# Two cross-attention layers on one core: key weights loaded in two parts, projections dealt out anew, and the layer-1-only units and the end in another order

## The chip, the cores and the metric

The kernel runs on one core of a Trainium2 chip. The metric is the device time of one execution in microseconds. Five engines work beside each other, each through its own instructions in order: TensorE (PE in the profile, with PEld for its weight loads), VectorE (DVE), ScalarE (ACT), GpSimd (POOL) and SyncE (SP), which here only issues DMAs. DMAs run in queues of the engines that issue them.

## The reference

Two attention layers follow each other, each with 20 heads of 16 channels, on x of shape 8 x 256 x 320 with a context of shape 8 x 256 x 512. A context of 256 rows has text rows and a few image rows (179 image rows in the first layer, 4 in the second), with projections of their own.

```python
# layer 0: text is enc[:, :77], ip is enc[:, 77:]
q = split(x @ Wq.T)
k, v = split(text @ Wk.T), split(text @ Wv.T)
k_ip, v_ip = split(ip @ Wk_ip.T), split(ip @ Wv_ip.T)
out = merge(attend(q, k, v)) + merge(attend(q, k_ip, v_ip))
x = out @ Wo.T + bo + x
# layer 1: text is enc[:, :252], ip is enc[:, 252:]
q = heads(x @ W_q)
probs_t = softmax(q @ k_t.T * scale)
text_out = probs_t @ v_t
qsem = l2norm(probs_t @ text)
fused = q @ k_ip.T * scale + 0.5 * (qsem @ l2norm(ip).T)
ip_out = (softmax(fused) * mask) @ v_ip
out = (text_out + ip_out) @ W_out + b_out + x
```

Layer 1 takes layer 0's result. All is float32.

## The kernel before, in words

**Tiling.** The 20 heads are taken as five quads of four heads (QUADS), for each of the eight batches. A unit of work n is one quad: n = 5 b + s for quad s of batch b in layer 0. Layer 1 follows six units behind (SHIFT), so for n from 6 to 39 a unit holds a quad of layer 0 and a quad of layer 1 (both_layers, L1078); units 40 to 45 hold layer 1 alone (layer_1, L1123); then l1_end (L863) finishes the last batch. Below, (b1, g4) is the unit with quad 4 of batch 1 in layer 0.

**Inside a unit.** Scores of four heads are 16 passes of TensorE (L342) into four PSUM tiles; the masked q that they take is made on GpSimd (qz, L332). VectorE takes the maxima (L483 for layer 0, L696 for layer 1), ScalarE the exps (L495, L711), TensorE transposes the probabilities (L380) back into the same PSUM tiles, and VectorE or ScalarE copies them out (et, L387). Layer 0 then multiplies with v (L513). Layer 1 multiplies, one unit later, with a Gram matrix of the context beside v (l1_values, L722, matmuls L735 and L738), in two PSUM tiles in turn; a product on VectorE (L742) gives the norm that l2norm needs, and a small copy (L746, "num") takes the values out. Only when both are done may the PSUM tile be written again. The scores on the four image rows are copied from the score tiles before the transposes overwrite them (aip, L691).

**Norms and the fused softmax.** Once a batch, l1_norm (L766) takes a square root on ScalarE (L773) and then calls a dummy Exp (L776), each of which brings a load of an activation table; l1_fused, l1_fused_exp (L794), l1_probs and l1_probs_T (L828, L835) follow.

**What sets the order.** PE, DVE, ACT and POOL are under a manual schedule: each engine executes in the order in which the program calls. The projections are dealt into the units by fillers(n, place) (L976): a table maps a pair (s, place) to a list of calls. In both_layers place 0 lies behind the exps of heads 0 and 1 of layer 0 and ahead of those of heads 2 and 3 (behind both where the flag late is set), place 1 behind the first two transposes, places 2 and 3 around the values of layer 1, place 4 between the exps of the two pairs of layer 1, place 5 and 6 among its transposes. In layer_1 places 2 and 3 follow the two halves of the first loop, place 4 the image scores, 5 and 6 the transposes. The projections are project_q (L275, with an ACT copy L282), project_k (L293; for the third column chunk ACT makes eight copies, L451 to L457), project_rows for v (L305), l1_gram (L604), l1_k (two ACT copies, L575 and L576) and the out-projections (L318).

**Loads.** At the start ACT's queue loads wq, wk, wkip, their last 64 columns again (load_tail), wv and wvip, in this order; SP's queue loads x and the context; the later weights come through POOL's queue (load_late).

**The end.** l1_end multiplies the last quad's values and finishes the last batch; its image softmax is taken in two parts, heads 0 to 15 (first) and 16 to 19 (last), then the sums of the heads are transposed (text), the image part is added (image), and the out-projection follows (project, L905).

## Time and profile before

| what | us |
|---|---|
| median of the runs before (3 runs: 904.05 to 906.41) | 904.2 |
| the profiled execution | 902.27 |
| its span, first to last instruction | 900.6 |
| PE busy | 867.4 |
| first scores of the first unit start | 14.89 |
| last unit with its end (866.89 to 900.60) | 33.71, PE busy 25.31 |
| a layer-1-only unit (832.02 to 842.41) | 10.39, PE busy 9.43 |

The mean granted clock of TensorE was 0.997. A line of the timeline gives the start, the duration, the engine, the line, the operation, the tiles written and read with their shapes, the count, and in brackets how long the engine was idle before it and what ended that. A line of the windows gives a stretch, its length, the busy time of PE, PEld, DVE, ACT and POOL with their counts, PE's granted clock, the busy share of the DMA engines and GB/s.

### The profile page before, as it was taken

The page shows a single profiled execution, that of the slowest core. Times are in us where ns is not written, and L with a number is a line of the kernel's source. Part 1 is how long each engine was busy: PE and PEld are TensorE (multiplying, and loading weights), DVE is VectorE, ACT ScalarE, POOL GpSimd, SP SyncE. Part 2 cuts the span into 40 slices and gives each one's busy share as a digit, 9 for nine tenths or more (in the row PEclk, how much of TensorE's full clock was granted, in tenths as well). Part 3 has the DMA queues.
Part 4 walks back from the last instruction along what each step waited for, and adds up shares of the span by engine and source line. Part 5 has one row for each costly group of instructions (what it writes and reads, how often), then busy time and mean ns, then how long its engine had stood idle before and what let it go on. Part 6 is the DMA issues. An engine that isn't in the chain of part 4 may idle for free.

```text
span 900.6 us, 18697 instructions
## 1 busy us (share of the span) xinstructions
PE 867.4 (96%) x6170; PEld 696.6 (77%) x6170; DVE 606.3 (67%) x2043; ACT 550.1 (61%) x2406; POOL 221.8 (25%) x397
## 2 busy tenths in 40 slices
PE   6999899999999999999999999999999999899996
PEld 4767678788777888788887788878877887678774
DVE  1454477767776777776777677776687767874664
ACT  3775666646654686556766468555775557745663
POOL 5522311213211232132221223212221223212201
PEclk9999999999999999999999999999999999999998
DMA  9500100001000100001001010001000100000000
GB/s 298 143 6 1 56 2 1 1 16 42 15 2 21 33 24 2 20 17 42 15 1 21 16 43 1 1 20 34 24 1 11 25 1 2 1 20 1 1 20 16
DMA packets 21072, 22.96 MB, mean 25 GB/s; under 512 B 5856, under 2 KB 20128, under 8 KB 20976
## 3 DMA queue, kind: packets, MB, share of 16 engines
q1 hardware_dynamic: 15072, 13.27, 5.8%
q10 hardware_dynamic: 4608, 4.38, 1.6%
q0 software_dynamic: 1296, 4.12, 1.5%
q8 instruction: 50, 0.82, 0.4%
q14 instruction: 46, 0.38, 0.1%
HBM read 18.31 MB, written 2.62 MB: 23 GB/s over the span
## 4 chain that ended last, share of the span: by engine, by line
PE 80%; ACT 6%; DVE 2%; issue 1%; POOL 0%; ACTq 0%; DVEq 0%
PE y L735 15%; PE sc L380 15%; PE sc L342 8%; PE v L305 8%; PE y L738 8%; PE k L293 6%; PE q L275 6%; PE p_o L318 5%; PE oT L513 4%; ACT e L495 2%; ACT e L711 2%; PE g L604 2%; PE p_aT_ps L311 1%; PE ipo L842 1%; PE o L533 1%
## 5 line engine op out<-in xcount | busy, mean ns | idle before, releaser
L495 ACT ACTIVATE e<-sc,nmx 128x77 f32<-128x77 f32 (+1 forms) x640 | 227.1, 411 | 57.5 <-DVE nmx L483 57.5
L711 ACT ACTIVATE e<-sc,nmx 128x252 f32<-128x252 f32 x320 | 147.0, 484 | 103.4 <-DVE aip L691 103.4
L735 PE MATMUL y<-gv,et 126*128 126x272 f32 x640 | 202.9, 398 | 5.0 <-ACT num L746 4.4
L742 DVE CUSTOM_DVE_ANT_0 e<-y,e 128x252 f32<-128x252 f32 x320 | 133.4, 418 | 108.2 <-PE y L738 96.4
L380 PE MATMUL sc<-ident,e 128*126 128x128 f32 (+1 forms) x1280 | 182.8, 275 | 11.8 <-ACT e L495 6.5
L483 DVE TENSOR_REDUCE nmx<-sc 128x2 f32<-128x154 f32 x320 | 109.6, 414 | 91.5 <-PE sc L342 91.5
L380 PEld LDWEIGHTS sc<-ident,e 128*126 128x126 f32 (+1 forms) x1280 | 148.1, 140 | 25.1 <-ACT e L495 12.5
L387 DVE COPY et<-sc 128x512 f32<-128x512 f32 (+1 forms) x222 | 149.9, 688 | 26.0 <-PE sc L380 16.8
L495 ACT ACTIVATION_READ_ACCUMULATOR e<-sc,nmx 128x1 f32 x640 | 159.7, 250 | 0.0
L738 PEld LDWEIGHTS y<-gv,et 126*128 126x128 f32 x640 | 121.1, 189 | 26.0
L738 PE MATMUL y<-gv,et 126*128 126x146 f32 x640 | 131.9, 288 | 0.0
L735 PEld LDWEIGHTS y<-gv,et 126*128 126x128 f32 x640 | 105.3, 191 | 22.7 <-ACT num L746 6.8
L548 POOL TENSOR_TENSOR attn<-o_sb 128x64 f32<-128x64 f32 x80 | 24.5, 327 | 396.9 <-DVE o_sb L538 357.0
L696 DVE TENSOR_REDUCE nmx<-sc 128x2 f32<-128x504 f32 x160 | 105.6, 673 | 24.2 <-PE sc L342 24.2
L387 ACT COPY et<-sc 128x512 f32<-128x512 f32 (+1 forms) x98 | 55.9, 587 | 75.4 <-PE sc L380 75.4
L342 PE MATMUL sc<-k,sc_qz 32*128 32x256 f32 x1152 | 83.4, 400 | 1.3 <-POOL sc_qz L332 0.8
L332 POOL TENSOR_SCALAR sc_qz<-q,quad_m 128x256 f32<-128x256 f32 x80 | 73.2, 926 | 10.2 <-ACT q L282 9.9
L342 PEld LDWEIGHTS sc<-k,sc_qz 32*128 32x128 f32 x1152 | 52.9, 184 | 24.7 <-issue 14.4
L711 ACT ACTIVATION_READ_ACCUMULATOR e<-sc,nmx 128x1 f32 x320 | 70.0, 219 | 0.0
L305 PE MATMUL v<-wv,encT 128*126 128x324 f32 (+1 forms) x192 | 58.1, 446 | 0.3 <-DMA wv<-in_WvT_dram 0.3
L318 PE MATMUL p_o<-wo,p_aT 128*128 128x320 f32 x180 | 52.8, 437 | 0.3 <-DVE p_aT L312 0.3
L746 DVE COPY num<-y 128x20 f32<-128x20 f32 x300 | 52.2, 174 | 0.0
(159 smaller groups left out, 1053.8 us busy)
## 6 DMA issues: line engine op xcount, KB each, us to landing
encT<-in_encT_dram SPq DMA_DIRECT2D x7, 512.0 KB
x<-in_x_dram SPq DMA_DIRECT2D x8, 320.0 KB
out_dram<-osb SPq DMA_DIRECT2D x15, 160.0 KB
xT<-in_xT_dram SPq DMA_DIRECT2D x7, 256.0 KB
texts<-in_encT_dram SPq DMA_DIRECT2D x6, 154.0 KB
xT<-in_xT_dram SPq DMA_DIRECT2D x7, 128.0 KB
vip_rows<-vipA SPq DMA_DIRECT2D x32, 25.0 KB
wk<-in_WkT_dram ACTq DMA_DIRECT2D x1, 640.0 KB
```

Source lines behind the costliest of these rows:

```text
L305: nc.tensor.matmul(ps, lhsT(k), w[:, k, :], start=(k == 0), stop=(k == NE - 1))
L318: nc.tensor.matmul(ps[:, :C], aT[:, m, :], w[:, m, :], start=(m == 0), stop=(m == NC - 1))
L342: nc.tensor.matmul(sc[j][:, half, :], qz[rows, half * P : (half + 1) * P], kT(j)[rows, :], start=True, stop=True,)
L380: nc.tensor.transpose(v[:, c, half, :], u["e"][x][:, i, half, t0 + c * tn : t0 + (c + 1) * tn], ident,)
L387: copy(u["et"][x][:tn, i].rearrange("p c n s -> p (c n s)"), ps)
L483: nc.vector.tensor_reduce(u["nmx"][x][:, j, :, a], u["sc"][2 * x + j][:, :, t0:t1], AX.X, ALU.max, negate=True,)
L495: nc.scalar.activation(u["e"][x][:, j, half, t0:t1], u["sc"][2 * x + j][:, half, t0:t1], AF.Exp, bias=u["nmx"][x][:, j, half, a : a + 1], ...
L696: nc.vector.tensor_reduce(u["nmx"][x][:, j, :], u["sc"][2 * x + j][:, :, t0 : t0 + TXT1], AX.X, ALU.max, negate=True,)
L711: nc.scalar.activation(u["e"][x][:, j, half, t0 : t0 + TXT1], u["sc"][2 * x + j][:, half, t0 : t0 + TXT1], AF.Exp, bias=u["nmx"][x][:, j, ...
L735: nc.tensor.matmul(y, et[:, 1 - odd, half, :], gv[0][:, g, full], start=True, stop=False)
L738: nc.tensor.matmul(y[:, into], et[:, odd, half, :], gv[1][:, g, part], start=False, stop=True)
L742: nc.vector.tensor_tensor_reduce(e, y[:, g0 : g0 + TXT1], e, op0=ALU.mult, op1=ALU.add, scale=1.0, scalar=0.0, accum_out=r["n2"][:, half, ...
```

## The change

Six things change.

1. wk and wkip become two tiles each: columns 0 to 127, and the rest with the 64 columns that are loaded again. The first parts (256 KB each) come on ACT's queue right after wq; wv, wvip and the rest of wk and wkip are issued on SP's queue. Four matmuls on zeros (8 passes) and a dummy Exp are put at the start.
2. (b1, g4) takes the last v projection of batch 2 at place 4; in (b2, g0) the third part of q moves from place 1 to place 0 in its stead.
3. In batches 2, 4 and 6 the second half of the next batch's l0_q moves from (3, 4) to (4, 0).
4. In the last batch (b = 7) the second Gram matrix moves from (2, 1) to (2, 4), the third part of l0_k from (2, 2) to (3, 0), the second l1_v from (3, 0) to (4, 0), the first l1_k from (40, 4) to (3, 4) and the second from unit 41 to unit 40. The flag late holds there for s = 4 and no longer for s = 3.
5. In layer_1 the first loop goes head by head: maximum, exp, product, with the copies shared differently. The transposes of heads 0 and 1 come ahead of the values of head 2. In the last unit l1_den is called ahead of the values of head 3.
6. In l1_end the copies of the first two heads' values go to VectorE, a dummy Sqrt is called ahead of the last two heads' values, the text matmuls come later, and the last transposed probabilities are copied by two engines.

```diff
@@ -117,10 +117,10 @@
         n = min(C, t.shape[2])
         eng.dma_start(out=t[:, :, 0:n], in_=w[:, 0:n].rearrange("(k p) c -> p k c", p=P))
 
-    def load_tail(t, w, eng):
+    def load_part(t, at, w, c0, c1, eng):
 
         eng.dma_start(
-            out=t[:, :, C:], in_=w[:, C - HP :].rearrange("(k p) c -> p k c", p=P)
+            out=t[:, :, at : at + c1 - c0], in_=w[:, c0:c1].rearrange("(k p) c -> p k c", p=P)
         )
 
     def load_xT(b, eng):
@@ -149,7 +149,11 @@
     wo, wo1 = new_c("wo"), new_c("wo1")
 
 
-    wk, wkip = new_e("wk", again=HP), new_e("wkip", again=HP)
+
+    wk, wkip = [
+        [const.tile([P, NE, n], F32, tag=f"{name}{n}", name=f"{name}{n}") for n in (P, C + HP - P)]
+        for name in ("wk", "wkip")
+    ]
     wk1 = const.tile([P, NE, C - HP], F32, tag="wk1", name="wk1")
 
     wv, wvip, wv1 = new_e("wv"), new_e("wvip"), new_e("wv1", again=NIP)
@@ -158,12 +162,23 @@
     bo_b = const.tile([P, C], F32, tag="bo_b", name="bo_b")
     bo1_b = const.tile([P, C], F32, tag="bo1_b", name="bo1_b")
     load_c(wq, WqT, nc.scalar)
-    load_e(wk, WkT, nc.scalar)
-    load_e(wkip, WkipT, nc.scalar)
-    load_tail(wk, Wk1, nc.scalar)
-    load_tail(wkip, Wk1, nc.scalar)
-    load_e(wv, WvT, nc.scalar)
-    load_e(wvip, WvipT, nc.scalar)
+    load_part(wk[0], 0, WkT, 0, P, nc.scalar)
+    load_part(wkip[0], 0, WkipT, 0, P, nc.scalar)
+    load_e(wv, WvT, nc.sync)
+    load_e(wvip, WvipT, nc.sync)
+    for w, given in ((wk, WkT), (wkip, WkipT)):
+        load_part(w[1], 0, given, P, C, nc.sync)
+        load_part(w[1], C - P, Wk1, C - HP, C, nc.sync)
+
+    zeros = work.tile([P, S], F32, tag="qz", name="zeros", bufs=2)
+    nc.vector.memset(zeros, 0.0)
+    ps = mm_tile("zeros")
+    for i in range(4):
+        nc.tensor.matmul(ps[:, :S], zeros[:, :P], zeros, start=True, stop=True)
+
+    one = small.tile([P, 1], F32, tag="one", name="one", bufs=1)
+    nc.vector.memset(one, 0.0)
+    nc.scalar.activation(one, one, AF.Exp)
 
     ident = const.tile([P, P], F32, tag="ident", name="ident")
     make_identity(nc, ident)
@@ -208,6 +223,8 @@
 
     def columns(w, k, m):
 
+        if isinstance(w, list):
+            w, m = (w[0], 0) if m == 0 else (w[1], m - 1)
         return w[:, k, m * P : (m + 1) * P]
 
     twice(wq)
@@ -690,9 +707,9 @@
         ip = 0 if u["t0"][x] else TXT1
         copy(bat[u["b"]]["aip"][:, :, h, :], sc[:, :, ip : ip + NIP])
 
-    def l1_max(u, x, image=True):
+    def l1_max(u, x, image=True, heads=range(2)):
         t0 = u["t0"][x]
-        for j in range(2):
+        for j in heads:
             nc.vector.tensor_reduce(
                 u["nmx"][x][:, j, :],
                 u["sc"][2 * x + j][:, :, t0 : t0 + TXT1],
@@ -703,9 +720,9 @@
             if image:
                 l1_image_scores(u, x, j, nc.vector.tensor_copy)
 
-    def l1_exp(u, x):
+    def l1_exp(u, x, heads=range(2)):
         t0 = u["t0"][x]
-        for j in range(2):
+        for j in heads:
             h = QUADS[u["g"]][1][2 * x + j]
             for half in range(NH):
                 nc.scalar.activation(
@@ -763,6 +780,11 @@
         nc.vector.reciprocal(by_head(r, "rden1", b)[:, :, hs], den)
         nc.vector.tensor_tensor(by_head(r, "nrm", b)[:, :, hs], den, den, ALU.mult)
 
+    def table(func):
+
+        one = small.tile([P, 1], F32, tag="one", name="one", bufs=1)
+        nc.scalar.activation(one, msk[:, 0:1], func)
+
     def l1_norm(b, hs=ALL):
         r = bat[b]
         n2 = r["n2"][:, :, hs]
@@ -771,9 +793,7 @@
         nc.vector.scalar_tensor_tensor(nrm, nrm, EPS2, n2, ALU.mult, ALU.max)
 
         nc.scalar.activation(nrm, nrm, AF.Sqrt, scale=1.0 / SEM_SCALE**2)
-
-        one = small.tile([P, 1], F32, tag="one", name=f"one_{b}", bufs=1)
-        nc.scalar.activation(one, msk[:, 0:1], AF.Exp)
+        table(AF.Exp)
 
     def l1_fused(b, hs=ALL, eng=nc.gpsimd):
         r = bat[b]
@@ -818,7 +838,7 @@
                 ALU.mult,
             )
 
-    def l1_probs_T(b, hs=ALL, ps=None):
+    def l1_probs_T(b, hs=ALL, ps=None, shared=False):
         r = bat[b]
 
         rows = hs.stop * NIP
@@ -832,7 +852,11 @@
             )
         if "pT" not in r:
             r["pT"] = small.tile([H * NIP, NH * P], F32, tag="pT", name=f"pT_sb_{b}", bufs=1)
-        nc.vector.tensor_copy(r["pT"][:rows], ps[:rows, : NH * P])
+        if shared:
+            for copy, cols in ((nc.vector.tensor_copy, slice(0, P)), (nc.scalar.copy, slice(P, 2 * P))):
+                copy(r["pT"][:rows, cols], ps[:rows, cols])
+        else:
+            nc.vector.tensor_copy(r["pT"][:rows], ps[:rows, : NH * P])
 
     def l1_attn(b):
         r = bat[b]
@@ -871,8 +895,9 @@
         def tile(j, name):
             return ps_sc.tile([P, NH * S], F32, tag=f"sc{j}", name=f"end_{name}")
 
-        def values(j, half):
-            l1_values(u, j, (half,), nc.scalar.copy)
+        def values(j, copy):
+            for half in range(NH):
+                l1_values(u, j, (half,), copy)
 
         def chunk(t, m):
             return t[:, CH[m] : CH[m] + P]
@@ -911,27 +936,23 @@
             for half in range(NH)
         ]
         o = [tile(2 + half, f"o_{half}") for half in range(NH)]
-        l1_den(b)
         l1_norm(b, first)
-        values(0, 0)
         l1_text(b, first)
-        values(0, 1)
+        values(0, nc.vector.tensor_copy)
         l1_fused(b, first)
-        values(1, 0)
-        values(1, 1)
+        values(1, nc.vector.tensor_copy)
         l1_fused_exp(b, first)
-        sums = tile(0, "aT")
-        text(sums, (0, 1))
-        values(2, 0)
-        values(2, 1)
+        table(AF.Sqrt)
+        values(2, nc.scalar.copy)
         l1_probs(b, first)
-        values(3, 0)
-        values(3, 1)
+        values(3, nc.scalar.copy)
         l1_norm(b, last)
         l1_text(b, last)
         l1_probs_T(b, first, tile(1, "pT"))
         l1_fused(b, last, nc.vector)
         l1_fused_exp(b, last, nc.vector)
+        sums = tile(0, "aT")
+        text(sums, (0, 1))
         image(sums, (0, 1), first)
         keep(sums, (0, 1))
         sums = mm_tile("end_aT2")
@@ -940,7 +961,7 @@
         project(0, 0)
         project(0, 1)
         project(1, 0)
-        l1_probs_T(b, last, tile(1, "pT2"))
+        l1_probs_T(b, last, tile(1, "pT2"), True)
         project(1, 1)
         image(sums, (2,), last)
         keep(sums, (2,))
@@ -1050,6 +1071,25 @@
                 },
             )[n]
             plan = {(s, at): f for at, f in plan.items()}
+        if b % 2 == 0 and b >= 2 and ahead < B:
+
+            plan[3, 4] = [(l0_q, ahead, (0,))]
+            plan[4, 0] = [(l0_q, ahead, (1,)), (l0_k, ahead, 0)]
+        if (b, s) == (1, 4):
+            plan[4, 4] = [(l0_v, ahead, 2)]
+        if (b, s) == (2, 0):
+            plan[0, 0], plan[0, 1] = plan[0, 1], []
+        if b == B - 1:
+
+            plan[2, 1] = [(l1_den, old), (l1_norm, old)]
+            plan[2, 2] = []
+            plan[2, 4] = [(l1_gram, now, 1), (l1_fused, old)]
+            plan[3, 0] = [(l0_k, now, 2)]
+            plan[3, 4] = [(l1_k, now, 0)]
+            plan[4, 0] = [(l1_v, now, 1)]
+        if b == B:
+            plan[0, 4] = [(l1_k, last, 1)]
+            plan[1, 4] = []
         for f, at, *args in plan.get((s, place), ()):
             if 0 <= at < B:
                 f(at, *args)
@@ -1082,7 +1122,7 @@
             l0_max(u0, pair)
         l0_exp(u0, 0)
 
-        late = n > NQ and n % NQ == 3
+        late = n > NQ and n % NQ == (3 if n < N0 - NQ else 4)
         if late:
             l0_exp(u0, 1)
         fillers(n, 0)
@@ -1131,21 +1171,21 @@
         if (n + 1 - SHIFT) % NQ:
             qz[1] = queries(1, n + 1)
         for pair in range(2):
-            l1_max(u1, pair, False)
-            l1_values(v1, pair, (0,), nc.scalar.copy)
-            l1_exp(u1, pair)
-            l1_values(v1, pair, (1,))
+            for j, copy in ((0, nc.vector.tensor_copy), (1, nc.scalar.copy)):
+                l1_max(u1, pair, False, (j,))
+                l1_exp(u1, pair, (j,))
+                l1_values(v1, pair, (j,), copy)
             fillers(n, 2 + pair)
         for head in range(4):
             l1_image_scores(u1, head // 2, head % 2, nc.scalar.copy)
         fillers(n, 4)
-        part(l1_values, v1, 2)
-        for head in range(4):
-            if head == 2:
-                fillers(n, 5)
-            part(l1_transposed, u1, head, nc.scalar.copy)
-        part(l1_values, v1, 3)
-        fillers(n, 6)
+        for pair in range(2):
+            for head in (2 * pair, 2 * pair + 1):
+                l1_transposed(u1, head, nc.scalar.copy)
+            if n == N0 + SHIFT - 1 and pair:
+                l1_den(B - 1)
+            part(l1_values, v1, 2 + pair)
+            fillers(n, 5 + pair)
         return None, u1
 
     l0_q(0, (0, 1))
```

## The prediction

> **What bounds the kernel now.** I read the page's busy shares first, then the chain of waits, then TensorE's timeline unit by unit, then the other engines' timelines where TensorE waits, and last the windows with the granted clock.
>
> ```profile
> PE 867.4 (96%) x6170; PEld 696.6 (77%) x6170; DVE 606.3 (67%) x2043; ACT 550.1 (61%) x2406; POOL 221.8 (25%) x397
> PE 80%; ACT 6%; DVE 2%; issue 1%; POOL 0%; ACTq 0%; DVEq 0%
> ```
>
> TensorE (PE) is busy 96% and is 80% of the chain that ended last. It idles 33 us of 900.6: about 8 before the first scores, 8 in the last unit and the end, the rest in small waits. No part of the change takes matmuls away, so it can win only these waits, and only where it makes no new ones. The four places:
>
> ```profile
> 12.86 1.48 PE L293 MATMUL k<-encT,wkip 128*128 128x179 f32 x8 [1.35 <-DMA wkip<-in_WkipT_dram]
> 14.89 1.15 PE L342 MATMUL sc<-k,sc_qz 32*128 32x256 f32 x16 [0.55 <-ACT k L445]
> ...
> 165.53 0.66 PE L380 MATMUL sc<-ident,e 128*126 128x128 f32 x4 [1.03 <-ACT e L711]
> ...
> 784.12 0.66 PE L380 MATMUL sc<-ident,e 128*128 128x128 f32 x4 [1.55 <-ACT e L495]
> ...
> 839.10 1.97 PE L380 MATMUL sc<-ident,e 128*126 128x128 f32 x16 [0.20 <-ACT aip L691]
> ...
> 880.97 0.72 PE L735 MATMUL y<-gv,et 126*128 126x272 f32 x2 [1.86 <-ACT num L746]
> ```
>
> The ends of matmuls are modelled, so an idle time is short by about 0.17. I therefore count waits by starts: a value product (L735 and L738) takes 0.70 from start to start, the transposes of one head 0.44, scores 1.08.
>
> **The head.** Now k waits for wk, then for wkip (12.86), and the first scores start at 14.89. After it, k needs two parts of 256 KB where 640 KB each were needed. The two queues share the engines packet by packet; with wv's packets beside them I put the second part at 11.3, so scores at about 13.35: -1.55, and the wait of 0.27 for wv goes (wv is no longer behind 640 KB of wkip): -1.85 in all. Bounds: 0 if wv's packets take the whole gain, -3.3 if nothing shares the queue. The 8 passes on zeros and the early dummy Exp stand in idle time; q (5.15 to 9.61) isn't last, since its copy ends at 12.6 and k's scores wait for k's copy at 14.37. If that cover went, the table load would cost its 1.28.
>
> **Second batch.** In (b1, g4) 165.53 follows 164.09 by 1.44 instead of 0.24, and the next head waits 0.46 more: 1.66 of wait take the moved v projection (8 passes, 2.25): +0.5. In (b2, g0) the 2.25 go; the six q passes (1.30) move up into that place; the exps, which give the first transposes no earlier than 3.6 after the scores, hold back the rest: -1.05. Together -0.55 (bounds -1.2 and +0.2).
>
> **Even batches (2, 4, 6).** Half of the 12 q passes, 1.30, leave g3, where the second head's exp (done at 249.53) then lets transposes start 0.9 earlier. They land in g4, ahead of transposes that wait 0.49 at 259.61 and 0.20 at 261.00: +0.55 net. So -0.35 a batch, -1.05 (bounds -2.5 and +0.3).
>
> **Last batch.** In g2, ACT's chain (two table loads, et copy to 755.92) holds the L1 scores as before; the k copies no longer stand before the L1 exps, and the gram (0.88) fills the wait of 0.87: -0.5. In g3, k takes the place of v: its 8 ACT copies now stand between the exps of heads 0,1 and those of heads 2,3, since "late" no longer holds here.
>
> ```profile
> 755.82 0.30 ACT L451 COPY k<-k 64x179 f32<-64x179 f32 x1
> ...
> 757.54 0.25 ACT L457 COPY k1c<-kt 64x77 f32<-64x77 f32 x1
> ```
>
> That is 755.82 to 757.79, 1.97 us. The exps of heads 2,3 end 1.97 later; the transposes of head 3, now at 771.19, can't come before 772.9: +1.7. The l1_k projection (1.70) fills 1.67 of wait behind the L1 scores, and its two copies (0.56) delay two exps: +0.2. In g4 the moved l1_v (2.28) fills 1.92 of wait: +0.35. Sum +1.75 (bounds -0.5 and +3).
>
> **The layer-1-only units.** Here I expect the loss. In the unit at 832.02 (10.39 long) both products of head 2 are issued before the transposes, which start at +7.08; behind them stand 1.8 of transposes and two products, 3.2. After it, all four products of heads 2 and 3 stand behind the first transposes: 1.8 + 4 x 0.70 = 4.6. To break even the transposes must start 1.4 earlier. They need the copy of head 0's image scores (L691), which stays on ACT behind all eight exps. The maxima (0.63 each) now alternate on DVE with products (0.35, with the copy 0.47): first maximum at +1.2, its successor held until product 0 is there (+2.1), the last ends at about +5.3; two exps 0.90, one copy, the image copy: transposes at +6.5, 0.5 earlier, not 1.4. So +0.9 a unit. In the unit at 832.02 ACT is held by table loads until 835.14 (+3.1), so transposes come at +7.2: +1.4. The unit at 821.10 loses 1.70 of k passes and this wait with them: +0.15. The unit at 854.10 has out-projections that fill: +0.7. With 842.41 (+0.9) that is +3.15 (bounds -1 if the maxima aren't held up, and +5).
>
> **The end** (with the unit at 866.89). Gone are the wait of 1.86 at 880.97, whose ACT copy stood behind Sqrt and two table loads, and the second Sqrt load at 889.01:
>
> ```profile
> 879.36 1.28 ACT L776 ACT_TABLE_LOAD   x1
> ...
> 889.01 1.28 ACT L773 ACT_TABLE_LOAD   x1
> ```
>
> Followed step by step from the scores: transposes +6.5 and products of head 3 to +11.1, first Sqrt +12.6, Exp table to +14.1, first fused exp +16.0, Sqrt preloaded to +17.6 (values of head 3 wait for the ACT copies behind it, +16.0 to +17.9), last Sqrt +20.3, last fused exp +22.0 where it was 891.93 (+25.0). So -2.9, the unit's own +0.9 included (bounds -4.5 and -0.5).
>
> **The clock.** One dip is in this trace, in the granted-clock column next to last but two:
>
> ```profile
> 878.83:882.24 3.41, 1.55 (x9) 1.17 (x8) 1.45 (x7) 1.86 (x5) 1.64 (x4) 1.00 0.02 7
> 882.24:885.65 3.41, 3.41 (x15) 3.17 (x14) 0.80 (x5) 0.66 (x3) 0.41 (x1) 0.50 0.00 0
> ...
> 773.01:776.42 3.41, 2.38 (x24) 1.60 (x23) 3.19 (x13) 1.27 (x6) 1.81 (x5) 1.00 0.01 2
> 11.85:15.26 3.41, 1.85 (x16) 1.61 (x20) 0.00 (x0) 1.11 (x3) 2.56 (x3) 1.00 1.19 297
> ```
>
> After a stretch with 1.55 us of PE work in 3.41 the clock is 0.50 for the next 3.41; after 1.85 and after 2.38 it isn't. So some 1.75 of idle in 3.4 us brings a dip, and a dip costs 3.41 x 0.5 = 1.7 where PE sets the pace. The new units have about 2.2 of idle in 3.4 (1.0 ahead of the last product of head 1, whose buffer now is freed by an ACT copy behind two exps, and 1.3 ahead of the transposes), the unit at 832.02 2.9. What decides is where the stretches fall: by the span of starts that catch 1.75, chances of 0.36, 0.57, 0.36 and 0.36 for the units at 821.10, 832.02, 842.41 and 866.89; 0.5 for the end's wait of 1.9, and 0.45 for g3 of the last batch (idle 1.9 at its third head). That is 2.6 dips, some only partly paid: I take +4.2 (bounds 0 and +10, six of 1.7).
>
> The Trainium skill ("TensorE: Matmul & The Clock Gate", Part 1 and "Why this matters for your kernels") has the gate go to half clock only after a whole idle window of about 3.4 us and asks for no gaps over some 3 us. The row at 878.83 disagrees, with a gap of 2.0 and 1.55 of work. By the page no new dip would come, and the sum below would be 4.2 less.
>
> **Sum.** -1.85 - 0.55 - 1.05 + 1.75 + 3.15 - 2.9 = -1.45; with the dips +2.75. The profiled execution took 902.27 (span 900.6 and 1.7 around it), so 905.0. The median of the runs is 904.2, 1.93 above; that puts the median after at 907.0. Less than 0.3% (2.7 us: 901.5 to 906.9) can't be told from no change.
>
> **Rivals.**
> - *No dips* (-1.45): 902.7. For it: one dip only in 900 us; against: no other stretch past the start has as little work as the new units would have.
> - *Faster*: the per-head order works. The first exp starts 1 us earlier (one maximum ahead of it, not two and a product), ACT gets through early and the layer-1 units stay as long as now; no dips: 904.2 - 1.45 - 3.15 = 899.6. It decides once transposes start before +5.7. Against it, the maxima alternate with products, each of which waits for PE.
> - *Slower still*: dips in five or six places, since a dip makes the next stretch longer but not the waits shorter; 902.7 + 5.5 x 1.7 = 912. It is over +0.3% from the third dip on.
> - *The head gains nothing* since wv's packets alternate with wkip's: 1.85 more on any of these.
>
> **Chances.** Forecast (two or three dips) 0.45, no dip or one 0.27, faster 0.18, five or six dips 0.10; the head's failure is spread over them. Faster than 901.5: the faster case and a third of the no-dip case, where the head or the end brings more, 0.27. Slower than 906.9: the last case and two thirds of the forecast, 0.40. Within: 0.33. The range of 898.5 to 911.5 takes in all cases but their outer bounds.
>
> **What would show it.** Head: first scores near 13.35. g3 of the last batch: 19.3 long instead of 17.34, with PE waiting for exps of heads 2,3. Layer-1 units: transposes near +6.5 and lengths of 11.3 to 11.8. Dips: stretches of clock 0.50 between 820 and 880. End: no table load in the last 15 us but one for Exp. It is wrong if those units stay at 10.4, or the clock stays at 1.00 with idle stretches of 2 us in the trace.

## The result, and the profile after

The change made the kernel slower: 912.63 us median (911.19 to 914.39) against 904.12, a ratio of 1.0098 with a 95% interval of 1.0076 to 1.0121. The forecast was 907.0, slower, with a range up to 911.5. The profiled execution after has a span of 911.0 (before 900.6).

From here on, "the unit at" gives the start in the trace of before, and a unit lasts from its scores to the next unit's. The lines of the code have moved: scores are L359 after, transposes L397, exps L512 and L728, products L752 and L755, the image copy L708.

TensorE is as busy as before in share, and what it waits for has grown. From the page of the kernel after, the busy times and the chain:

```profile
PE 876.6 (96%) x6178; PEld 702.1 (77%) x6178; DVE 605.7 (66%) x2049; ACT 550.7 (60%) x2408; POOL 222.0 (24%) x397
PE 77%; ACT 8%; DVE 2%; issue 1%; POOL 0%; ACTq 0%; DVEq 0%
```

PE's 9.2 us more of busy time are 3.8 of passes on zeros (1.24 to 5.02) and, for the rest, passes that ran at half clock; q, at full clock earlier, takes 1.6 less (2.90 for 4.46). ACT's share of the chain is 8% where it was 6%. TensorE's timeline after, the places that answer to the lines shown of before:

```profile
12.80 2.76 PE L310 MATMUL k<-encT,wkip 128*128 128x179 f32 x8 [1.57 <-DMA wkip<-in_WkipT_dram]
16.11 2.09 PE L359 MATMUL sc<-k,sc_qz 32*128 32x256 f32 x16 [0.55 <-ACT k L462]
...
773.16 0.66 PE L397 MATMUL sc<-ident,e 128*128 128x128 f32 x4 [1.76 <-ACT e L512]
...
792.73 0.54 PE L866 MATMUL ipo<-vip,pT_sb 80*128 80x320 f32 x1 [1.78 <-ACT gv L649]
...
845.78 0.72 PE L752 MATMUL y<-gv,et 126*128 126x272 f32 x2 [1.24 <-ACT num L763]
847.74 1.53 PE L397 MATMUL sc<-ident,e 128*126 128x128 f32 x8 [0.98 <-ACT aip L708]
...
898.05 0.72 PE L752 MATMUL y<-gv,et 126*128 126x272 f32 x2 [1.57 <-ACT num L763]
```

k still waits for wkip until 12.80 (12.86 before), so in this run the new order of the loads won nothing there, and then it takes 2.76 where it took 1.48. In quad 3 of the last batch the transposes of head 2 wait for the exps behind the k copies. In quad 4 the second image matmul waits 1.78 for copies of gv, which the prediction did not have. In the layer-1-only units there are two waits where three smaller ones were. Only the end waits less.

Where the 10.4 us are, unit by unit (us, after minus before, and without the half clock where another profile has the unit so):

| place | forecast | measured | without half clock |
|---|---|---|---|
| start of the trace to the third unit's scores | -1.85 | +3.49 | -0.3 to -0.7 |
| (b1, g4) and (b2, g0) | -0.55 | -0.56 | |
| even batches, three | -1.05 | -1.14 | |
| last batch, quad 2 | -0.5 | -0.23 | |
| last batch, quad 3 | +1.9 | +2.25 | |
| last batch, quad 4 | +0.35 | +3.88 | +2.2 |
| unit at 801.53 | 0 | +0.69 | |
| units at 821.10, 832.02, 842.41, 854.10 | +3.15 | +4.94 | +3.26 |
| unit at 866.89 with the end, to the last matmul | -2.9 | -2.81 | -1.15 |
| half clocks, wherever | +4.2 | in the rows above | |

The last column: the start from three kernels below that keep the new start (37.45, 37.66 and 37.89 to the third unit's scores, before 38.16; their wkip also came 0.6 to 1.3 earlier than here); quad 4 is 23.22 in after_no_zeros; the unit at 832.02 is 11.73 in after_late_as_before; the end of before is 28.53 in before_kept_busy, where no half clock falls into it.

The windows with the granted clock, of the kernel after (columns as before: stretch, length, PE, PEld, DVE, ACT, POOL, clock, DMA share, GB/s):

```profile
8.57:11.98 3.41, 1.09 (x8) 0.97 (x8) 0.00 (x0) 0.34 (x1) 2.97 (x4) 1.00 1.09 344
11.98:15.39 3.41, 2.59 (x8) 2.29 (x8) 0.00 (x0) 0.00 (x0) 3.41 (x7) 0.50 1.15 307
15.39:18.80 3.41, 2.86 (x18) 1.81 (x18) 0.61 (x2) 0.37 (x1) 0.66 (x2) 0.50 1.04 340
18.80:22.22 3.42, 3.42 (x8) 2.21 (x7) 2.13 (x7) 2.91 (x16) 0.76 (x2) 0.50 1.05 341
...
769.74:773.15 3.41, 1.62 (x11) 1.31 (x10) 2.01 (x9) 3.34 (x17) 1.51 (x4) 1.00 0.00 0
773.15:776.57 3.42, 3.38 (x22) 2.77 (x23) 1.68 (x7) 1.94 (x9) 0.90 (x1) 1.00 0.00 0
...
790.22:793.64 3.42, 1.64 (x8) 0.93 (x7) 1.50 (x5) 2.46 (x16) 2.24 (x4) 1.00 0.00 0
793.64:797.05 3.41, 3.41 (x14) 3.04 (x13) 1.74 (x6) 0.00 (x0) 0.16 (x1) 0.50 0.00 0
...
844.84:848.25 3.41, 1.48 (x9) 1.19 (x10) 1.89 (x8) 3.05 (x18) 0.47 (x1) 1.00 0.00 0
848.25:851.66 3.41, 3.41 (x14) 2.94 (x13) 0.52 (x3) 1.17 (x2) 0.52 (x1) 0.50 0.01 2
```

A stretch is one of the 3.41 us between the places where the clock can change, and its work is PE's busy time in it. The stretches with 1.09, 1.48 and 1.64 us of work are each followed by one at 0.50; the one with 1.62 at 769.74 is not, so the amount of work alone does not decide. At the start the half clock lasts three stretches: after 2.59 and 2.86 us of work it goes on, after 3.42 it ends.

### The profile page after: what moved, and what is told of

Its sections match the earlier page's. It is cut to its first block, busy times and chain, and to the rows that moved or that the text cites. A ratio compares the mean times of both kernels' runs of the same rounds, so it can differ in the third digit from the quotient of the medians.

```text
span 911.0 us, 18726 instructions
## 1 busy us (share of the span) xinstructions
PE 876.6 (96%) x6178; PEld 702.1 (77%) x6178; DVE 605.7 (66%) x2049; ACT 550.7 (60%) x2408; POOL 222.0 (24%) x397
## 4 chain that ended last, share of the span: by engine, by line
PE 77%; ACT 8%; DVE 2%; issue 1%; POOL 0%; ACTq 0%; DVEq 0%
PE y L752 15%; PE sc L397 14%; PE sc L359 8%; PE y L755 8%; PE v L322 8%; PE k L310 6%; PE p_o L335 5%; PE q L292 5%; PE oT L530 4%; ACT e L512 3%; ACT e L728 3%; PE g L621 2%; PE p_aT_ps L328 1%; PE ipo L866 1%; PE o L550 1%
## 5 line engine op out<-in xcount | busy, mean ns | idle before, releaser
L512 ACT ACTIVATE e<-sc,nmx 128x77 f32<-128x77 f32 (+1 forms) x640 | 227.1, 411 | 58.2 <-DVE nmx L500 58.2
L728 ACT ACTIVATE e<-sc,nmx 128x252 f32<-128x252 f32 x320 | 147.3, 484 | 118.7 <-DVE aip L708 105.4
L752 PE MATMUL y<-gv,et 126*128 126x272 f32 x640 | 203.9, 400 | 7.2 <-ACT num L763 6.3
L397 PE MATMUL sc<-ident,e 128*126 128x128 f32 (+1 forms) x1280 | 184.7, 276 | 12.6 <-ACT e L512 6.3
L397 PEld LDWEIGHTS sc<-ident,e 128*126 128x126 f32 (+1 forms) x1280 | 149.0, 141 | 26.4 <-ACT e L512 12.8
L512 ACT ACTIVATION_READ_ACCUMULATOR e<-sc,nmx 128x1 f32 x640 | 159.3, 249 | 0.0
L755 PEld LDWEIGHTS y<-gv,et 126*128 126x128 f32 x640 | 121.8, 190 | 26.4
L755 PE MATMUL y<-gv,et 126*128 126x146 f32 x640 | 132.4, 289 | 0.0
L752 PEld LDWEIGHTS y<-gv,et 126*128 126x128 f32 x640 | 105.5, 192 | 23.8 <-ACT num L763 7.9
L359 PE MATMUL sc<-k,sc_qz 32*128 32x256 f32 x1152 | 84.7, 404 | 1.9 <-ACT et L404 0.8
L359 PEld LDWEIGHTS sc<-k,sc_qz 32*128 32x128 f32 x1152 | 53.4, 185 | 25.9 <-issue 16.2
L728 ACT ACTIVATION_READ_ACCUMULATOR e<-sc,nmx 128x1 f32 x320 | 69.9, 219 | 0.0
L322 PE MATMUL v<-wv,encT 128*126 128x324 f32 (+1 forms) x192 | 60.1, 459 | 0.0
```

Of the source, the lines that this page charges most:

```text
L322: nc.tensor.matmul(ps, lhsT(k), w[:, k, :], start=(k == 0), stop=(k == NE - 1))
L359: nc.tensor.matmul(sc[j][:, half, :], qz[rows, half * P : (half + 1) * P], kT(j)[rows, :], start=True, stop=True,)
L397: nc.tensor.transpose(v[:, c, half, :], u["e"][x][:, i, half, t0 + c * tn : t0 + (c + 1) * tn], ident,)
L512: nc.scalar.activation(u["e"][x][:, j, half, t0:t1], u["sc"][2 * x + j][:, half, t0:t1], AF.Exp, bias=u["nmx"][x][:, j, half, a : a + 1], ...
L728: nc.scalar.activation(u["e"][x][:, j, half, t0 : t0 + TXT1], u["sc"][2 * x + j][:, half, t0 : t0 + TXT1], AF.Exp, bias=u["nmx"][x][:, j, ...
L752: nc.tensor.matmul(y, et[:, 1 - odd, half, :], gv[0][:, g, full], start=True, stop=False)
```

## The experiments

The theory after the result: four losses apart from each other, (a) the start's half clock, (b) the k copies in quad 3 of the last batch, (c) the l1_v copies in quad 4, which come late and hold one of two PSUM tiles, (d) the order in the layer-1-only units; and one gain, the end. The rivals stand in the expectations. Runs of one kernel differ by up to 6 us, and the differences go with the mean granted clock (96 runs of before: 900.3 to 901.1 at 0.999 or 1.0, 905.2 to 906.5 at 0.992), so each was run several times, and profiles are compared unit by unit.

### The start: no zeros, and zeros alone

after_no_zeros takes this out of the kernel after; before_plus_zeros puts it, with the dummy Exp, into before:

```diff
-    zeros = work.tile([P, S], F32, tag="qz", name="zeros", bufs=2)
-    nc.vector.memset(zeros, 0.0)
-    ps = mm_tile("zeros")
-    for i in range(4):
-        nc.tensor.matmul(ps[:, :S], zeros[:, :P], zeros, start=True, stop=True)
```

> The kernel after without its four matmuls on zeros (the early dummy Exp stays). Clock theory: the zeros bring TensorE to full clock before q, so q ends at 8.3 instead of about 9.7, the stretch from 8.6 to 12.0 holds only 1.1 us of work, and the clock is halved from 12.0 to 22.2. Without them q fills that stretch, the clock stays at 1.00 from about 8.6 on, k on the second part takes 1.5 instead of 2.76, the first scores start near 14.9 instead of 16.1, the first unit takes 11.7 instead of 14.4: 3.5 to 4 us less than the kernel after, about 908.8. Rival, the loads alone: wkip's part lands at 12.8 whatever the clock does, and the 3.5 us lost by the start of the third unit stay: 912.

Measured: 909.88 (907.71 to 911.75), 1.0076 [1.0049, 1.0103]. In the profile the first scores start at 14.23 with the clock at 1.00, the first unit takes 11.44, but then the third unit's scores wait 2.19 us for GpSimd. The forecast was 908.8.

> The kernel before with nothing but the four matmuls on zeros and the early dummy Exp put in. Clock theory: q at full clock ends near 8.3, the stretch behind it holds about 1.1 us of work in 3.4, the clock is halved from 12 on for two or three stretches: first scores 1 us later, first unit 2 to 3 us longer, in all 2.5 to 4 us slower than before. Rival: the warm clock helps q, k waits for its load as before, nothing or up to 0.5 us is won.

Measured: 906.0 (900.76 to 907.79), 1.0017 [0.9997, 1.0036]. The profile shows the mechanism that was expected: q ends at 8.2, k waits 2.18 and 1.38, the clock is halved from 12.5 to 19.3, the first unit takes 12.94. But 28 of 96 runs of before have a mean clock of 0.992 without any zeros; here 7 of 12 have 0.992 or less. A tendency, no proof.

### The kernel after once more, and TensorE kept busy

> The kernel after once more, for the spread of its runs beside the next three. The start theory (half clock at the start in nearly all of its runs, three stretches, 3.5 us) expects a mean clock of 0.988 to 0.991 in most runs and 911 to 914; if the half clock at the start comes and goes, runs near 907 with a clock of 0.996 or more are among them.

Measured: 910.9 (909.02 to 914.35), 1.0077 [1.0056, 1.0098]; clocks of 0.988 to 0.994, only two of six below 0.992 where most were expected. In this profile the half clock at the start lasts two stretches (12.64 to 19.46), not three. The ratio is that of after_no_zeros, so what the zeros cost is not settled: anything from 0 to 3 us.

before_kept_busy puts matmuls of no use into the two waits of before's start:

```diff
+    def keep_busy(n, name):
+        ps = mm_tile(name)
+        for i in range(n):
+            nc.tensor.matmul(ps[:, :S], wq[:, 0, :P], wq[:, 0, :S], start=True, stop=True)
...
+            if i and name == "k0_0" and m == 0:
+                keep_busy(3, "busy1")
...
     l0_q(0, (0, 1))
+    keep_busy(1, "busy0")
     l0_k(0, 0)
```

> The kernel before with matmuls of no use in the two waits for k's weights at the start (2 passes behind q, 6 between k's two parts, 1.7 us in all). Clock theory: the runs of before differ by 5.5 us since the half clock comes at the start in most of them; with the waits filled no stretch of 3.4 us there has less than 1.85 of work, so the runs with a clock of 0.992 and 0.996 go: median 901 to 902, 2 us less than before with more work. Rival: the half clock at the start comes from elsewhere (loads, or how the chip wakes up): same spread, 0.5 us slower or the same.

Measured: 902.35 (900.87 to 904.55), 0.9984 [0.9969, 0.9998]. Eleven of 12 runs have a clock of 0.998 or more, where 70 of 96 runs of before (12 of the 17 beside it) have less: more work, less time. So in before it is TensorE's idle time in the waits for k's weights that brings most of the half clock, and the runs of before differ mainly for this reason. Where it falls is seen in before_plus_end, further down, whose start is that of before:

```profile
10.07:13.48 3.41, 1.93 (x12) 1.41 (x12) 0.00 (x0) 1.88 (x2) 0.55 (x1) 1.00 1.21 293
13.48:16.89 3.41, 2.86 (x16) 2.37 (x18) 0.00 (x0) 0.37 (x1) 3.41 (x5) 0.50 1.08 342
```

In the kernel after, the same cause is likely but not shown: no run fills its waits alone, and loop_late_kept_busy, below, is no faster for the filling (896.88 against 896.87).

### The flag late, and the PSUM tile behind it

```diff
-        late = n > NQ and n % NQ == (3 if n < N0 - NQ else 4)
+        late = n > NQ and n % NQ == 3
```

> The kernel after with the flag late as before (s = 3 in every batch). Theory: in quad 3 of the last batch the eight k copies go behind all exps, so the wait of 1.76 for the exps of head 2 goes; in quad 4 the l1_v copies stand between the exps of the two pairs, so they free their PSUM tile some 3 us earlier, the wait of 1.78 of the second image matmul goes and the half clock of 793.6 to 797.1 (1.7) with it. Together 4 to 5 us less than the kernel after: about 908. Rival: the copies only move, and delay the L1 exps of quad 3 as they delayed those of quad 2 before: 1 us of it comes back, and the half clock falls elsewhere: 0 to 2 us less.

Measured: 904.65 (901.52 to 908.07), 1.0014 [0.9996, 1.0033]; some 6 to 8 us less than the kernel after, where 4 to 5 were expected. Quad 3 takes 17.63 instead of 19.59, quad 4 21.17 instead of 24.89. To tell the two apart, the next sets late in no unit of the last batch, so the k copies stay in their bad place:

```diff
-        late = n > NQ and n % NQ == (3 if n < N0 - NQ else 4)
+        late = NQ < n < N0 - NQ and n % NQ == 3
```

> The kernel after with the flag late set in no unit of the last batch: the k copies of quad 3 stay between the exps of the two pairs as in the kernel after, but the l1_v copies of quad 4 come between them too. Theory, two causes: quad 3 stays at 19.6 (the copies ahead of the exps of heads 2 and 3, 2.0), and quad 4 goes from 24.9 to 21.2, since l1_v's PSUM tile is free before the second image matmul asks for it (1.8) and no half clock follows there (1.7): 2 to 3.5 us less than the kernel after, 909 to 910.5. Rival, one cause: all of the loss hangs on the k copies of quad 3 and what they delay; quad 4 stays near 24: 912.

Measured: 907.08 (903.84 to 910.3), 1.0041 [1.0023, 1.0059]. Quad 3 stays at 19.60, quad 4 is 21.17, and its image matmuls run in one go from 788.59 without a wait. Two causes, as expected. The timeline of ACT in the kernel after shows the second:

```profile
791.82 0.29 ACT L512 ACTIVATION_READ_ACCUMULATOR e<-sc,nmx 128x1 f32 x1
791.91 0.39 ACT L648 COPY gv<-v 126x160 f32<-126x160 f32 x1
...
792.35 0.33 ACT L649 COPY gv<-v 126x40 f32<-126x40 f32 x1
```

The v projection of layer 1 leaves TensorE by 787.9, but with late set its four copies stand behind the last exp (791.82). Until 792.68 they hold one of the two PSUM tiles of mm_tile; the other goes to the first image matmul at 790.25, and the second, in line for the held one, waits until 792.73 (1.78 idle). The half clock of 793.64 follows this wait.

### The loop of the layer-1-only units

after_loop_as_before puts the old loop back into the kernel after, here its first half; the second half (values of head 2 ahead of the transposes) and the place of l1_den go with it:

```diff
         for pair in range(2):
-            for j, copy in ((0, nc.vector.tensor_copy), (1, nc.scalar.copy)):
-                l1_max(u1, pair, False, (j,))
-                l1_exp(u1, pair, (j,))
-                l1_values(v1, pair, (j,), copy)
+            l1_max(u1, pair, False)
+            l1_values(v1, pair, (0,), nc.scalar.copy)
+            l1_exp(u1, pair)
+            l1_values(v1, pair, (1,))
             fillers(n, 2 + pair)
```

> The kernel after with the loop of the layer-1-only units as before (maxima in pairs, values of head 2 ahead of the transposes; l1_den back in the end). Theory: the units of 11.2, 13.4, 12.5 and 13.6 go back to about 10.5, 10.4, 11.7 and 12.8, the half clock at 848 goes: 5 us less in these, and the last unit another 0.8: 906.5 to 907.5. Rival: the end's gain of 2.8 hangs on the new order (transposes of heads 0 and 1 early); it goes as well, and 2 to 3 us are left: 910.

Measured: 904.43 (900.86 to 906.36), 1.0008 [0.999, 1.0025], 6 to 8 us less than the kernel after. The four units are 10.39, 10.39, 11.69 and 12.79, as before but for the first (10.92 before, with k passes that have moved), the unit at 801.53 is 19.57 again, and the last with its end still takes 27.20 to the last matmul. The end's gain doesn't hang on the loop. after_values_first keeps the new loop and only moves the values of head 2 ahead of the transposes:

```diff
         fillers(n, 4)
+        part(l1_values, v1, 2)
         for pair in range(2):
             for head in (2 * pair, 2 * pair + 1):
                 l1_transposed(u1, head, nc.scalar.copy)
...
-            part(l1_values, v1, 2 + pair)
+            if pair:
+                part(l1_values, v1, 3)
             fillers(n, 5 + pair)
```

> The kernel after with one change in the loop of the layer-1-only units: the values of head 2 stand ahead of the transposes again, as before; maxima, exps and products still go head by head. Theory: the loss is the order of values and transposes (two products behind the first transposes), not the alternation on VectorE: the products fill the wait of 1.0 ahead of the transposes, which start at +6.5 to +7 as now; units of 9.9 to 10.4 where the kernel after has 11.2 to 12.5, and no dip there: 5 us less, 907. Rival: the alternation is what costs (each maximum behind a product): the transposes come later by what the two products take on VectorE, and 1 us or less is won.

Measured: 905.14 (903.12 to 908.26), 1.0016 [1.0, 1.0031]. The units at 832.02 and 842.41 take 10.99 and 11.80 (11.73 and 12.52 without half clock, 10.39 and 11.69 before): two thirds of their loss is won back, though not the 9.9 to 10.4 that was expected. The unit at 821.10 wins back only 0.16 (11.06 for 11.22), and that at 854.10 nothing (13.58). Against the old loop in after_loop_as_before the four units lose 3.8 in all, and 1.6 of it comes back. So the order of values and transposes is the larger part of the loss in two units, not over all four. Beside it stands a product that waits for an ACT copy behind two exps. TensorE's timeline of this kernel in the unit at 832.02 (here from 836.02), where before waits 0.48 and 0.28 ahead of products and 0.20 ahead of the transposes:

```profile
841.06 0.73 PE L752 MATMUL y<-gv,et 126*128 126x272 f32 x2 [1.23 <-ACT num L763]
842.94 0.73 PE L752 MATMUL y<-gv,et 126*128 126x272 f32 x2 [0.20 <-ACT num L763]
```

after_filled_waits leaves the order and puts two matmuls of no use into the wait:

```diff
         fillers(n, 4)
+        if n > N0:
+            ps = mm_tile(f"fill_{n}")
+            for i in range(2):
+                nc.tensor.matmul(ps[:, :S], ident, wq[:, 0, :S], start=True, stop=True)
```

> The kernel after with two matmuls more (four passes, 0.86 us) ahead of the transposes in units 41 to 45; their product goes nowhere. Clock theory: they fall into the wait of 1.0 and cost nothing there, and the stretch of 3.4 us no longer has 1.75 of idle, so no half clock comes in these units (13.4 at 840.7 becomes 11.7): 1 to 2 us less in the median than the kernel after, 911, though there is more work; the mean granted clock is higher by 0.002. Rival: idle time isn't what brings the half clock; the units stay as long or get longer by up to 0.3 each where the wait is shorter than the filling: 912.6 to 914.

Measured: 908.01 (905.64 to 911.01), 1.0051 [1.0032, 1.007], 2.9 to 4.6 us below the kernel after. In its timeline the filling stands in the wait and the transposes start at +7.0 after the scores (837.68), as in the kernel after (847.74 behind 840.74):

```profile
842.72 0.73 PE L752 MATMUL y<-gv,et 126*128 126x272 f32 x2 [1.23 <-ACT num L763]
843.29 0.41 PE L755 MATMUL y<-gv,et 126*128 126x146 f32 x2
843.54 1.03 PE L1185 MATMUL fill<-wq,ident 128*128 128x256 f32 x4
844.68 1.09 PE L397 MATMUL sc<-ident,e 128*126 128x128 f32 x8
```

The unit takes 11.72 instead of 13.41 and no stretch between 820 and 900 is at half clock. That fits the clock theory, but one profile does not prove it: in after_again, without any filling, the same unit takes 11.73, since there the half clock falls into the next. The unit at 854.10, which has no such wait, takes 14.44 instead of 13.58.

### The parts that were to win, alone in before

before_plus_end has the new l1_end, and before_plus_projections the moves in the second and the even batches; both as in the change.

> The kernel before with nothing but the new end (copies of the first two heads on VectorE, early Sqrt, text matmuls later, shared copy). Theory: the last unit with its end goes from 30.2 between scores and last matmul (28.5 without a half clock) to 27.2: 1.5 to 3 us less than before, about 902. Rival: the gain belongs to the half clock alone, which comes and goes in any case: under 0.5 us.

Measured: 900.0 (899.1 to 901.81), 0.9962 [0.9945, 0.9979]. The unit with the end takes 27.20 to the last matmul, 1.33 less than before without a half clock (28.53), so the gain is not the half clock alone. There are four table loads as before, but the second Sqrt load runs 16.0 us after the unit's scores instead of 22.1, ahead of the copies of the last two heads' values. The wait of 1.86 is gone; one of 1.57 at 887.05, for those copies, stands in its place.

> The kernel before with nothing but the moves of the v and q projections in the second and the even batches. Theory, from the units of the kernel after (+0.33, -0.89; -0.88 and +0.50 three times): 1.7 us less than before, about 902.2. Rival: such moves only trade waits; no difference.

Measured: 902.43 (899.31 to 902.8), 0.9979 [0.9963, 0.9995]. The moved units take what they take in the kernel after (17.90 and 24.38, 19.49 and 20.51), and no other unit past the start changed.

### The good parts together

> The kernel after with both the loop of the layer-1-only units and the flag late as before. If the two losses are apart, each undoing keeps its worth: at one clock the late flag is worth 4.7 and the loop 6: about 895.5 in runs without a half clock, and a median of 898 to 900 with the dips at the start (three stretches in most runs) left in. Rival: both remove the same dip or the same wait of ACT, so the second undoing brings only 1 to 2 more: 902 to 903.

Measured: 896.87 (896.01 to 898.97), 0.9925 [0.9908, 0.9943]. Both undoings keep their worth, and fewer runs than expected have a half clock at the start (898 to 900 was expected for the median).

> The same without the four matmuls on zeros. Clock theory: with the zeros 8 to 9 in 12 runs have half clock after the start, without them fewer; 2 to 3 us less in the median than with them: 896 to 897. Rival: where the free-running stretches fall at the start is chance, and the early zeros only help q: no difference in the median, within 1 us of the kernel with zeros.

Measured: 896.96 (896.19 to 899.63), 0.9921 [0.9904, 0.9938]: no difference from the zeros in this kernel.

> The kernel after with loop, flag late and the whole start (loads, zeros, dummy Exp) as before. Theory: the start of the kernel after brings 1 us at the first scores, but GpSimd, which issues the late loads and waits for them, gives the masked q of the third unit no earlier; 0.5 us of it is left: 897.4 without half clocks. Rival: with 5 of 6 runs of the loop-and-late kernel nearly free of half clocks, the old start, which has them in most runs, costs 2 to 4 more: 899 to 901.

Measured: 899.46 (897.26 to 899.6), 0.9949 [0.9932, 0.9967]. At full clock the two kernels differ by 0.6 to 1.4 us (896.01 and 896.71 against 897.26 to 897.44); the rest of the 2.6 is half clock at the old start. So the new start does win here. In the profiles its first scores come 0.98 earlier than in that of before (13.91 for 14.89), its third unit's 0.50 earlier; part of the gain is lost to a wait for GpSimd. Its timeline in after_loop_and_late_as_before, ahead of the third unit's masked q:

```profile
34.15 0.35 POOL L102 COPY wq<-wq 128x192 f32<-128x192 f32 x1 [3.04 <-DMA wq<-in_Wq_dram]
34.46 1.70 POOL L143 TENSOR_TENSOR x<-x,bo_b 128x320 f32<-128x320 f32 x2
36.10 0.61 POOL L565 TENSOR_TENSOR attn<-o_sb 128x64 f32<-128x64 f32 x2
36.68 0.93 POOL L349 TENSOR_SCALAR sc_qz<-q,quad_m 128x256 f32<-128x256 f32 x1
```

A copy waits for a late weight, the bias adds and the masked q queue behind it, and the third unit's scores wait 1.10 for it at 37.66. In before they wait 0.31. That this wait costs time in the end is read from the timeline, not tested.

> The kernel after with loop and flag late as before, and six passes of no use in each of the two waits for k's weights at the start. Clock theory: no half clock at the start in any run, 896 in all. Rival: the passes delay k (the first wait can be as short as 0.5 us): first scores up to 0.8 later, 897.

Measured: 896.88 (896.32 to 902.11), 0.9935 [0.9911, 0.9958]. The profile has no half clock at the start; two of 6 runs (900.68 and 902.11, clocks of 0.998 and 0.996) still differ by more than the forecast allows, and where they lost it wasn't seen.

The last also moves GpSimd's work one unit back:

```diff
         if n == 0:
             load_late()
+        if n == 1:
             twice(wkip1, wq1)
             load_resid(0)
```

> The same, with GpSimd's two copies that wait for late loads, and its bias adds of the first residual, one unit later. Theory: the third unit's masked q no longer stands behind them; the wait of 1.0 to 3.0 us ahead of the third unit's scores goes, 1 to 2 us less: 894.5 to 895. Rival: the wait goes to the fourth unit or later, where the copies and adds come then: no gain.

Measured: 895.98 (895.88 to 896.1, 4 runs), 0.991 [0.9892, 0.9928], the fastest and the steadiest of all, and faster than before and after. The wait that it was to remove wasn't there in either profile of this pair, so its 0.9 us are not shown to come from that.

## Why the prediction was wrong

The direction was right and the size was not: +2.75 forecast for the profiled execution, +10.4 measured in span. Two terms of the sum failed, the head and the last batch's quad 4, and most of the half clock fell where none was counted, at the start. Of the 7.7 us between forecast and result some 3 are half clock, by an estimate from the table: it cost about 7.2 (3.9 at the start, with the late load of this run in it, and 1.7 in each of two units) where +4.2 was forecast. The rest is in the head (1.4), quad 4 (1.85), the unit at 801.53 (0.69) and small differences. By the prediction's own steps:

- **The head** failed, by 5.3 us. It was put at -1.85, with scores at 13.35 and the zeros and the dummy Exp free of cost, and measured +3.49. Two things went wrong. k's waits (1.86 and 1.57) leave a stretch with 1.09 us of work, the clock fell to half for 10.2 us, and k, scores and v took 1.8 to 1.9 times as long. The rule that I had read off the trace for the layer-1 units (some 1.75 us of idle in 3.41) I did not lay on the start, where I took the idle time as free cover. And the loads came later than the 11.3 I had put: k's second part at 12.80 in this run, at 11.4 to 12.2 in others, so that even at full clock first scores come at 13.5 to 14.2. The bound in the prediction, packets of wv between those of the keys, would do this; no run separates it. Behind it stood a wait that I hadn't looked at, in GpSimd's queue.
- **The last batch's quad 4** failed: +0.35 forecast, +2.2 and a half clock of 1.7 measured. I counted TensorE's passes and ACT's copies, and not what the copies hold: a PSUM tile, one of two. after_no_late_in_last shows that the late copies are the cause; that it is by the tile is read from the timelines.
- **Quad 3** was right: +1.9 forecast, +2.25, by the k copies ahead of the exps of heads 2 and 3. **Quad 2** gave 0.23 of 0.5.
- **The layer-1-only units** were right in size: units +0.30, +1.34, +0.83, +0.79 without half clock (forecast +0.15, +1.4, +0.9, +0.7), transposes at +6.5 in two of them (forecast +6.5) and at +7.0 for +7.2 in the unit at 832.02. The mechanism, products behind transposes that come too little earlier, holds for part: after_values_first takes it away and wins back 1.6 of 3.8, nothing in the unit at 854.10. The rest goes with the product that waits for ACT's copy, which the prediction has only under the clock: the unit at 854.10 has no wait before and this one, of 0.72, after. The unit at 801.53 was put at 0 and lost 0.69: a product there waits 0.63 for the same kind of ACT copy.
- **The end** was right in mechanism and size: -2.81 for -2.9, of which 1.66 is before's own half clock. The first fused exp comes at +15.9 (forecast +16.0) and the last at +21.8 (+22.0). The second Sqrt load is not gone but moved, to 896.43, off the path.
- **Second and even batches** were right to 0.1.
- **The clock**: two dips past the start in the profile, near places that were named (832.02, which had the highest chance, and the last batch, there one quad later than named), where 2.6 were forecast. The rule behind the chances was too simple: it put the edge between 1.55 and 1.85 us of work, from three rows, and the runs since have half clock after 1.93 and none after 1.62. The Trainium skill ("TensorE: Matmul & The Clock Gate", Part 1) has the clock halved after at least one idle window of about 3.4 us. The rows at 8.57, 790.22 and 844.84 disagree, and they decide: each had work in it, and half clock followed.
- The faster rival fell, since transposes start at +6.5 where +5.7 was its point. The case with five or six dips (912) came out near the measured time by luck: there are five stretches at half clock before the last matmul, but three of them are at the start, where it had none.

## What to carry to other kernels

Waits at a start or in a tail are not free cover: where an engine's clock follows its work, as TensorE's does here, add up the work of each stretch around every wait that a change makes. When copies are moved behind other work on their engine, ask which buffer they hold, and who is next in line for it. When products are moved behind another step, the step must come earlier by all that now stands behind it.

## What the runs showed of the hardware

- TensorE's clock is halved for stretches of 3.41 us, or several in a row, on a grid that lies differently in each profile (the first half clock begins at 11.98 in the kernel after and at 12.64 in the same kernel once more).
- Little work in a stretch brings it, but there is no one threshold. In the 18 traces, up to the last matmul, half clock followed all nine full-clock stretches with at most 1.56 us of work and none with more than 2.18. In between both happened: 1.64 (after, 790.22), 1.70 (after_again, 852.32) and 1.93 (before_plus_end, 10.07) brought it, 1.62 (after, 769.74) and 1.70 (before_kept_busy, 877.53) did not.
- Getting back takes more busy time than staying: at half clock, stretches with 2.59 to 3.10 us (after and after_loop_as_before) did not restore it, 3.19 (before_plus_zeros) and 3.41 did.
- The spread of the runs of before goes with it: of 96 runs the 28 with a mean clock of 0.992 took 905.2 to 906.5, the ten with 0.999 or 1.0 took 900.3 to 901.1.
- Useless matmuls in a wait can save time: 902.35 for 903.66 (0.9984 [0.9969, 0.9998]) at before's start.
